# Eighteen runs of transposes in an attention stage taken from TensorE and done by VectorE in blocks of 32 and through DRAM

## The chip, the core and the metric

The program runs on one core of a Trainium2 chip. The core has a matrix engine (TensorE, PE in the profile, its weight loads PEld), a vector engine (VectorE, DVE), an activation engine (ScalarE, ACT), a general engine (GpSimd, POOL) and SyncE (SP), which here issues DMAs and relays semaphores. Every engine takes its own instructions strictly in the order in which they were written. The metric is device time in microseconds (us) of one execution; the number for the kernel before is the median of three runs.

## The reference, cut to what matters

The computation is four layers of a residual network over x, float32, 8 blocks of 512 tokens by 128 features. Each layer is an attention-like part and a feed-forward part, each behind a layer norm. The change is in the stage that does the attention of layer 2, together with what was folded into that stage: the expert layer of layer 2 (on the first 1024 tokens) and the whole of layer 3.

```python
# layer 2, attention: 16 heads of 64, softmax over the QUERIES (axis 2)
q, k, v = (einsum('bsd,hpd->bhsp', x, w) + bias for each)
scores  = einsum('bhqp,bhkp->bhqk', q, k) / 8
attn    = softmax(scores, axis=2)
ctx     = einsum('bhqk,bhkp->bqhp', attn, v)
out     = ctx.reshape(..., H * P) @ l_w.T + l_b
# layer 3, first part: a causal depthwise convolution of 21 taps
h_hatt  = conv(x, taps)
out     = x @ W1 + h_hatt @ W2 + bias
# layer 3, second part: both operands of every product rounded to FP4 in blocks of 16
gate, y = fp4(x) @ fp4(w_gate).T, fp4(x) @ fp4(w_up).T
out     = fp4(silu(gate) * y) @ fp4(w_down).T

x = x + L2_attn(layernorm(x));  x = x + L2_ffn(layernorm(x))
x = x + L3_attn(layernorm(x));  x = x + L3_ffn(layernorm(x))
```

Every product needs its input with the features on the partitions, while x lies with the tokens on the partitions. So each normalised block has to be transposed ("turned") before the product: 512 x 128 as four squares of 128.

## The kernel before, in words

`late()` (from L1403) holds the stage. It consists of 64 *frames*, n = 0 to 63: frame n is one pair of heads of one block of 512 tokens, eight frames to a block, so block 0 has frames 0 to 7, block 1 frames 8 to 15, and so on. In one frame the engines do, in the order written:

- `scores(n, 0)`: TensorE makes the scores of key tiles 0 and 1 (two PSUM pairs, `bank2`, of which there are two). VectorE takes the maxima (`nm`, L1626), ScalarE the exponentials (`ex`, L1632).
- `context(n - 1)`: TensorE multiplies the previous frame's exponentials with the weighted values.
- `scores(n, 1)`: key tiles 2 and 3. They need the two PSUM pairs back, that is, the exponentials of tiles 0 and 1 done.
- `project(n)`: TensorE makes queries, keys and values for later frames and the output product of the frame before; VectorE and ScalarE move `k`, `v` and `q` out of PSUM, `k` and `q` from the two banks of the pool "one".
- `weigh(n, 0)` and `weigh(n, 1)`: VectorE takes the reciprocals of the sums (`sm`, L1646), GpSimd scales the values.

Everything else is hung into these frames by a plan written out by hand. `at(frame, hook, f)` puts a step at one of six places of a frame; steps of one place run in the order in which they were entered, first the layer-2 inputs, then layer 3 of block 0, of block 1, and so on. The places: S between the score products of key tile 1; P between the exponentials of the two tiles; V after the first scores and before `context`; G before the second scores; D before the projections; E at the end of the frame, after `weigh(n, 1)` and before the next frame's scores. 

`planned(b, f0)` enters layer 3 of block b from frame f0 on, with f0 = 13, 20, 27, 34, 41, 48, 56 for blocks 0 to 6; block 7 comes in `end()`. Blocks 0 to 4 are "wide". Its steps before the change, by frame counted from f0: 0 statistics of the norm; 1 the norm (`scale`, ScalarE, four instructions) and the turn (`turn_`); 2 to 4 the taps of the convolution on VectorE, ScalarE and GpSimd; 5 its product, its sum into x and the second norm's statistics; 6 the second norm; 8 and 9 the rounding of x (`quant_x1`, `quant_x2`) and its turn (`turn_x`); 10 to 13 the gate and up products of the four tiles (`gate_steps`, hook S); 11 to 14 the rounding of h in two halves, each of 704 columns (`quant_h1`, `quant_h2`); 12 and 14 the turning of h (`blocks_h`), 13 and 15 its fetch (`fetch_h`), 16 the last product (`down`, three squares a tile). So in any run of seven frames, work of three blocks overlaps.

A *turn* is four transposes on TensorE against a unit matrix into one PSUM bank of the pool "one", and a copy of that bank (128 x 512) to SBUF, by ScalarE for activations and by VectorE for the weights. It stands at hook E, between `project` and the next frame's scores.

The turning of h is already done the other way: VectorE transposes 128 x 704 in blocks of 32 (L2151), four DMAs on the queue of SyncE write the blocks to their places in a DRAM array (L2155), and a frame later two DMAs bring back the rows (L2163).

SyncE has a second role. `mark` (L1518 to L1522) puts an instruction into SyncE's queue that waits for a matmul and then releases a later one; `project` has two of them in a frame and `gate_steps` one. A matmul that has such a mark ahead of it cannot start before SyncE has worked off all that stands before the mark.

## Time and profile before

| | |
|---|---|
| median of 3 runs | 1401.11 us (1397.96 to 1403.28) |
| the profiled execution | 1403.74 us, its span 1402.0 us |
| first and last exponential of the 64 frames start at | 514.3 us and 1337.8 us |
| seven frames of the middle, 938.70 to 1026.75 us | 88.05 us |
| TensorE, VectorE, ScalarE, GpSimd busy | 95%, 72%, 72%, 46% of the span |
| granted TensorE clock | 0.995 |

Times in the profile count from the start of the span. The busy share of TensorE is of modelled ends: the product of one group starts while the one before still drains, so that the start of the next group tells more than the end of this one. A line of the time order reads: start, duration, engine, line of the kernel, operation, out<-in, shape, count, and in brackets how long the engine had been idle and who ended that. The queue of SyncE is SPq. A DMA's "us to landing" is from its issue to the semaphore that tells its arrival.

### The profile page before, as it was taken

The page shows a single profiled execution, that of the slowest core. Times are in us where ns is not written, and L with a number is a line of the kernel's source. Part 1 is how long each engine was busy: PE and PEld are TensorE (multiplying, and loading weights), DVE is VectorE, ACT ScalarE, POOL GpSimd, SP SyncE. Part 2 cuts the span into 40 slices and gives each one's busy share as a digit, 9 for nine tenths or more (in the row PEclk, how much of TensorE's full clock was granted, in tenths as well). Part 3 has the DMA queues.
Part 4 walks back from the last instruction along what each step waited for, and adds up shares of the span by engine and source line. Part 5 has one row for each costly group of instructions (what it writes and reads, how often), then busy time and mean ns, then how long its engine had stood idle before and what let it go on. Part 6 is the DMA issues. An engine that isn't in the chain of part 4 may idle for free.

```text
span 1402.0 us, 33150 instructions
## 1 busy us (share of the span) xinstructions
PE 1336.6 (95%) x12967; PEld 711.6 (51%) x12967; DVE 1013.3 (72%) x2148; ACT 1011.9 (72%) x2052; POOL 647.0 (46%) x756
## 2 busy tenths in 40 slices
PE   7889999999989999999999999999999999999997
PEld 3762222222267655547446545555555555545576
DVE  6775655676467768863784678879788797887876
ACT  6859999999978555665685686777777767667632
POOL 6756666666632533340463354353443534424432
PEclk9999999999999999999999999999999999999999
DMA  5029999888581010021211101101001010010000
GB/s 179 1 40 130 132 136 133 128 124 126 79 271 31 28 40 24 17 82 30 82 32 43 45 1 23 23 10 33 20 18 27 9 33 20 12 33 9 2 8 16
DMA packets 84714, 78.15 MB, mean 56 GB/s; under 512 B 35821, under 2 KB 76685, under 8 KB 80078
## 3 DMA queue, kind: packets, MB, share of 16 engines
q1 hardware_dynamic: 82828, 72.10, 27.3%
q0 software_dynamic: 1152, 2.36, 0.6%
q8 instruction: 103, 1.69, 0.5%
q10 hardware_dynamic: 578, 1.57, 0.3%
q14 instruction: 53, 0.43, 0.1%
HBM read 59.03 MB, written 16.97 MB: 54 GB/s over the span
## 4 chain that ended last, share of the span: by engine, by line
PE 50%; ACT 23%; DVE 18%; DMA 3%; issue 3%; POOL 2%; SPq 1%; DVEq 0%; ACTq 0%; POOLq 0%
PE ps L250 39%; PE ps L1553 8%; ACT hm L568 7%; ACT ex L1632 6%; DVE nm L1626 5%; ACT hm L567 3%; ACT prod L2020 2%; DMA gs<-gates 2%; DMA gates<-eq 1%; PE ps L2203 1%; DVE fa L1392 1%; DVE acc L2006 1%; ACT h L388 1%; DVE s L729 1%; DVE fa L1376 1%
## 5 line engine op out<-in xcount | busy, mean ns | idle before, releaser
L1632 ACT ACTIVATE ex<-ps,nm 128x512 f32<-128x512 f32 x512 | 345.2, 687 | 173.6 <-DVE nm L1626 171.2
L1626 DVE TENSOR_REDUCE nm<-ps 128x2 f32<-128x1024 f32 x256 | 301.2, 1211 | 44.0 <-PE ps L250 43.6
L250 PE MATMUL ps<-q,k 64*64 64x512 f32 (+1 forms) x2240 | 259.5, 568 | 7.4 <-ACT ex L1632 5.4
L250 PE MATMUL ps<-ex,vs 128*64 128x512 f32 x1024 | 233.8, 598 | 1.1 <-DVE sm L1646 1.1
L1647 POOL TENSOR_TENSOR vs<-v,sm 128x256 f32<-128x256 f32 x128 | 78.6, 614 | 297.5 <-DVE sm L1646 268.2
L586 POOL TENSOR_TENSOR acc<-acc,pr 128x512 f32<-128x512 f32 x119 | 166.5, 1399 | 105.7 <-DVE pr L580 97.4
L1553 PE MATMUL ps<-xt,blob_a 64*64 64x512 f32 x912 | 208.0, 589 | 0.3 <-SPq L1520 0.2
L568 ACT ACTIVATE hm<-ps,blob_f 128x1536 f32<-128x1536 f32 x128 | 196.2, 1533 | 0.0
L580 DVE SCALAR_TENSOR_TENSOR pr<-ps,blob_f,gs 128x512 f32<-128x512 f32 x120 | 90.0, 750 | 88.2 <-PE ps L250 71.7
L250 PEld LDWEIGHTS ps<-q,k 64*64 64x64 f32 x2240 | 74.9, 132 | 151.0 <-ACT ex L1632 77.5
L250 PE MATMUL ps<-h,w 32*128 32x512 f32 x1024 | 147.4, 639 | 1.5 <-ACT hm L567 0.6
L250 PEld LDWEIGHTS ps<-ex,vs 128*64 128x64 f32 x1024 | 68.0, 136 | 153.7 <-issue 128.1
L250 PE MATMUL ps<-hm,w 128*32 128x512 f32 x1024 | 136.2, 604 | 3.2 <-DVE pr L580 3.0
L2021 POOL TENSOR_TENSOR acs<-acs,prod 128x512 f32<-128x512 f32 x96 | 124.1, 1292 | 23.9 <-ACT prod L2020 19.4
L1553 PE MATMUL ps<-blob_a,ct 64*64 64x128 f32 x1824 | 118.6, 269 | 0.0
L1553 PE MATMUL ps<-blob_a,xt 64*64 64x128 f32 x1824 | 118.5, 269 | 0.0
L1553 PEld LDWEIGHTS ps<-blob_a,ct 64*64 64x64 f32 x1824 | 106.1, 133 | 0.0
L1632 ACT ACTIVATION_READ_ACCUMULATOR ex<-ps,nm 128x1 f32 x512 | 105.0, 205 | 0.0
L1553 PEld LDWEIGHTS ps<-blob_a,xt 64*64 64x64 f32 x1824 | 103.0, 133 | 0.0
L567 ACT ACTIVATE hm<-ps,blob_f 128x512 f32<-128x512 f32 x128 | 88.0, 687 | 18.6 <-PE ps L250 18.5
L250 PEld LDWEIGHTS ps<-h,w 32*128 32x128 f32 x1024 | 40.7, 183 | 109.0 <-ACT hm L567 92.2
L1553 PEld LDWEIGHTS ps<-xt,blob_a 64*64 64x64 f32 x912 | 61.6, 132 | 32.3 <-issue 28.7
(375 smaller groups left out, 2219.9 us busy)
## 6 DMA issues: line engine op xcount, KB each, us to landing
gs<-gates SPq DMA_DIRECT2D x256, 128.0 KB, 6.7
ht<-turned_h SPq DMA_DIRECT2D x20, 180.0 KB, 2.9
turned_h<-hb SPq DMA_DIRECT2D x40, 88.0 KB, 2.3
blob_f<-in_f SPq DMA_DIRECT2D x1, 2560.0 KB, 9.3
blob_a<-in_a SPq DMA_DIRECT2D x1, 2056.0 KB, 15.4
x<-in_x SPq DMA_DIRECT2D x8, 256.0 KB, 5.6
gates<-eq SPq DMA_DIRECT2D x8, 256.0 KB, 5.6
slots_in<-nought SPq DMA_DIRECT2D x8, 256.0 KB, 4.3
```

The costliest lines, as they stand in the source:

```text
L250: nc.tensor.matmul(out_, lhs, rhs, start=start, stop=stop)
L388: nc.scalar.activation(hk, hk, AF.Sigmoid, bias=bi[:, k : k + 1], scale=sc[:, k : k + 1])
L567: nc.scalar.activation(hm[:, 0, :], p1, AF.Gelu, bias=bias)
L568: nc.scalar.activation(hm[:, 1:, :], p3, AF.Gelu, bias=bias)
L580: nc.vector.scalar_tensor_tensor(pr, po, f0["b2"][:, e : e + 1], gs, ALU.add, ALU.mult)
L586: nc.gpsimd.tensor_tensor(acc[:, b, :], acc[:, b, :], pr, ALU.add)
L1553: ins = nc.tensor.matmul(*args, **kw).ins
L1626: nc.vector.tensor_reduce(nm, ps, AX.X, ALU.max, negate=True)
L1632: nc.scalar.activation(ex[kt][:, i, :], ps[:, i, :], AF.Exp, bias=nm[:, i : i + 1], accum_out=sm[:, kt, i : i + 1],)
L1647: nc.gpsimd.tensor_tensor(vs[:, tiles, :, :], vs_[n][:, tiles, :].rearrange("p j (i n) -> p j i n", i=2), sm[:, tiles, :].unsqueeze(3).to_ ...
L2020: nc.scalar.activation(p, src, AF.Copy, scale=w)
L2021: nc.gpsimd.tensor_tensor(t["acs"], t["acs"], p, ALU.add)
```

## The change

Eighteen turns lose their transposes on TensorE and their copy out of PSUM: the inputs of layer 2 for blocks 1 to 7, the inputs of layer 3 for blocks 2 to 4, the rounded x of blocks 0 to 4, and the three rounded weights. In their place VectorE transposes the source in place in blocks of 32, four DMAs on SyncE's queue write it to a new DRAM array, and, one frame later (two for the weights), a DMA on the same queue fetches it.

```diff
+            def in_blocks(src):
+                nc.vector.transpose(src, src)
+                far = tc.dram_tile([P, TB], F32, name=f"turned{len(fars)}")
+                fars.append(far)
+                to = far.rearrange("(c r) (j a s) -> a r j c s", c=4, j=J, a=4)
+                for a in range(4):
+                    nc.sync.dma_start(
+                        to[a],
+                        src[32 * a : 32 * (a + 1), :].rearrange("r (j c s) -> r j c s", j=J, c=4),
+                    )
+                return far
...
+                def blocks():
+                    t["far"] = in_blocks(t["xn"].rearrange("p j d -> p (j d)"))
+
+                def fetch():
+                    nc.sync.dma_start(dst(), t["far"])
...
+                def blocks_x():
+                    t["far"] = in_blocks(t["xq"])
+
+                def fetch_x():
+                    t["xt"] = xt = tile_("xt", block("xt3", 2))
+                    nc.sync.dma_start(xt, t["far"])
...
-                plan = [
-                    (1, "V", s.stats) if b == 1 else (0, "E", s.stats),
-                    (1, "G", s.scale),
-                    (1, "E", s.turn_),
+                more = 2 if b < NB - 4 else 0
+                if 2 <= b <= 4:
+                    plan = [
+                        (-1, "E", s.stats),
+                        (0, "G", s.scale),
+                        (0, "E", s.blocks1),
+                        (1, "E", s.fetch1),
+                    ]
...
-                    (6, "E", s.quant_x1) if early else (z - 2, "V", s.quant_x1),
-                    (z - 1, "V", s.quant_x2),
-                    (z - 1, "E", s.turn_x),
+                if wide:
+                    plan += [
+                        (z - 3, "V", s.quant_x1),
+                        (z - 2, "V", s.quant_x2),
+                        (z - 2, "E", s.blocks_x),
+                        (z - 1, "E", s.fetch_x),
+                    ]
...
-                    (h_ + 4, "V", lambda: s.quant_h2(1)),
+                    (h_ + 4 + more, "V", lambda: s.quant_h2(1)),
...
-                        (z + 4, "E", lambda: s.blocks_h(1)),
-                        (z + 5, "E", lambda: s.fetch_h(1)),
-                        (z + 6, "E", s.down),
+                        (z + 4 + more, "E", lambda: s.blocks_h(1)),
+                        (z + 5 + more, "E", lambda: s.fetch_h(1)),
+                        (z + 6 + more, "E", s.down),
...
-                at(n + 1, "E", turn_)
+                for i, f in enumerate(t_["in turn"]):
+                    at(n + 1 + i, "E", f)
...
-                    at(frame + 1, "E", lambda name=name: turned_w(name))
+                    at(frame + 1, "E", lambda name=name: raw.update({(name, 0): turned_w(name)}))
+                    at(frame + 3, "E", lambda name=name: fetch_w(name, raw[name, 0]))
```

(z is 10 for the wide blocks.) Around these, three more things move. For layer 3 of blocks 2 to 4 the statistics and the norm come one frame earlier, into frames f0 - 1 and f0. The rounding of x of the wide blocks comes one frame earlier, into frames f0 + 7 and f0 + 8. And for blocks 0 to 3 the second half of h is rounded, turned, fetched and multiplied (`down`) two frames later: rounding and `blocks_h(1)` in f0 + 16 instead of f0 + 14, `down` in f0 + 18 instead of f0 + 16. The statistics and norms of the layer-2 inputs stay where they were.

## Prediction

> **What bounds the kernel now.** I read the page first (busy shares, chain), then the seven frames that repeat in the middle, then the time order of each engine at the places that the change touches.
>
> ```profile
> span 1402.0 us, 33150 instructions
> PE 1336.6 (95%) x12967; PEld 711.6 (51%) x12967; DVE 1013.3 (72%) x2148; ACT 1011.9 (72%) x2052; POOL 647.0 (46%) x756
> PE 50%; ACT 23%; DVE 18%; DMA 3%; issue 3%; POOL 2%; SPq 1%; DVEq 0%; ACTq 0%; POOLq 0%
> ...
> 953.86:966.03 12.17, 12.17 (x136) 5.98 (x134) 10.75 (x24) 8.92 (x25) 3.07 (x7) 1.00 0.12 33
> 966.03:977.73 11.70, 11.61 (x136) 5.96 (x134) 10.86 (x23) 8.92 (x25) 5.27 (x8) 1.00 0.13 20
> 977.73:988.23 10.50, 10.41 (x130) 5.61 (x128) 8.05 (x13) 8.80 (x24) 3.10 (x7) 1.00 0.22 50
> 988.23:1002.83 14.60, 14.15 (x176) 9.27 (x176) 11.26 (x16) 10.57 (x25) 4.60 (x5) 1.00 0.07 21
> ```
>
> The four stretches are frames 33 to 36, from first exponential to first exponential: length, then PE, PEld, DVE, ACT, POOL busy (instructions), clock, DMA. TensorE fills 97 to 100% of each; VectorE 77 to 93%, ScalarE 72 to 84%. In block 3's count (f0 = 34) they are f0 - 1 to f0 + 2. So TensorE is the bound, but a chain of maxima, exponentials and freed PSUM runs close behind it: what is added to VectorE or ScalarE is hidden only by a microsecond or so.
>
> ```profile
> 972.91 0.49 PE L1553 MATMUL ps<-blob_a,xt 64*64 64x128 f32 x6
> 973.51 0.63 PE L1469 MATMUL ps<-blob_c,xn 128*128 128x128 f32 x4
> 974.07 1.95 PE L250 MATMUL ps<-q,k 64*64 64x512 f32 x16
> ...
> 997.09 2.94 PE L250 MATMUL ps<-wd,ht 120*128 120x128 f32 x24 [0.45 <-DVE k L1515]
> 999.87 0.60 PE L2086 MATMUL ps<-blob_c,fa 128*128 128x128 f32 x4
> 1000.40 1.52 PE L250 MATMUL ps<-q,k 64*64 64x512 f32 x16
> 1001.74 0.46 PE L2203 MATMUL ps<-wt_gate,xt 64*64 64x352 f32 x2
> 968.69 0.60 ACT L1667 COPY ct<-ps 128x512 f32<-128x512 f32 x1
> 969.16 1.66 ACT L1451 ACTIVATE xn<-x,nb,rs 128x128 f32<-128x128 f32 x4
> 970.71 0.40 ACT L1964 ACTIVATE tapw<-blob_l 128x128 f32<-128x128 f32 x1
> 971.14 0.69 ACT L1632 ACTIVATE ex<-ps,nm 128x512 f32<-128x512 f32 x1
> ...
> 975.29 2.03 SPq L2155 DMA_DIRECT2D turned_h<-hb  x4
> L2151 DVE STREAM_TRANSPOSE hb<-h x10: 877/880/882, 861.0 to 1240.1; 128x704 f32<-128x704 f32 x10
> DMA to landing us min/median/max: 1.9/2.3/3.8
> rows<-back SPq DMA_DIRECT2D x7, 256.0 KB, 2.7
> ```
>
> To see: a turn (L1469, L2086) takes 0.53 to 0.56 us from its start to the next product's. In frame 34 ScalarE goes from copy to norm to tap weight to exponential without a gap. Four block writes hold SyncE's queue 2.03 us (L2155). The gate product of a block begins 1.34 us after the scores of its frame (1001.74 against 1000.40).
>
> **Term 1, TensorE's turns: -13.3 us.** After a projection a turn costs 0.56 and some 0.27 more (the last projection group starts 0.60 before the turn, 0.33 before scores where no turn stands): 0.83. After `down` only 0.53. Layer-2 inputs 7 x 0.83 = 5.85; layer-3 inputs 3 x 0.83 = 2.5; rounded x 0.9 + 4 x 0.53 = 3.0; three weights about 0.64 each = 1.9. With them go 15 ScalarE copies of 0.58; the three weight copies on VectorE (0.49 to 0.53) are replaced by transposes.
>
> **Term 2, VectorE's transposes: 0 by themselves.** 704 columns take 0.88; the rounding's rows of 352, 512 and 704 columns (0.53, 0.69, 0.89) give 1.0 ns a column, so 0.68 for 512 (bounds 0.49, a copy of 352 columns, and 0.88). At hook E VectorE waits up to 0.75 for the next scores in the lighter frames, and these now come 0.83 earlier; I charge the heavy frames in term 4.
>
> **Term 3, a DMA that comes too late: 4 x 5.3 = +21.2 us.** `fetch_x` stands at E of f0 + 9, one frame before its reader: the gate product in f0 + 10. With `down` moved, `blocks_h(1)` of the block before (its f0 + 16) falls into the same hook E, and it was entered first. This is so in frames 29, 36, 43 and 50; the built order of SyncE's queue has there four `turned_h<-hb`, then `xt<-turned`, then the gate's mark. So `fetch_x` waits behind four writes, which wait for a VectorE transpose at the very end of the frame. From the end of the frame's last exponential, e: `sm` 0.17, `hb` 0.88, four issues 2.05, then the fetch. No row has this 256 KB fetch; I take `rows<-back`, 256 KB from DRAM, 2.7 (bounds 2.2, the `out<-x` store, and 3.5, the slowest `ht` fetch). Landing is at e + 5.9 to 6.4, the longer where VectorE is late with `v`. TensorE wants the gate product at about e + 0.8, when `q` (0.70 on ScalarE after e) has freed its bank; `down` and `turn_x`, 3.3 us before, no longer stand ahead of it. So it stands 5.3 us (4.3 to 6.1), in order, and with it the rest of the scores, `context`, the tanh and the exponentials behind it. Nothing of that is cover: the reader is TensorE.
>
> Block 0's fetch (frame 22) has no writes before it, is issued in the middle of the projection and lands about when the gate wants it: 0. `fetch1` has a frame of convolution start to wait for it (f0 + 2, V), behind four writes of `blocks_x`: 0 to 0.5, taken 0. The eight writes of f0 hold SyncE about 4.1 us; the next marks are those of `project`, some 7 us after E: 0.
>
> **Term 4, VectorE and ScalarE in f0 - 1 to f0 + 1 of blocks 2 to 4: 3 x 2.2 = +6.6 us.** The statistics (0.84 + 0.36 + 0.17, overlapped 1.23) now stand before the next maxima in f0 - 1, where another 1.23 already stands: exponentials 1.2 later, second scores about 1.0 later. In f0 ScalarE, which has no gap, gets a second norm of 1.65: the second exponentials start at about 973.9 instead of 971.14 (frame 34), and the scores of the next frame need the PSUM that they free. Four exponentials (2.7) and the last tile's scores (0.85) later these scores end at 977.5 instead of 975.95, although the turn is gone. The rounding of h that leaves f0 (2.85 us of VectorE) and the copies that go give about 1.0 back in f0 + 1. So of two turns (-1.66) nothing is left, and 0.55 is added: 2.2. Bounds 0 (all in the shade of TensorE) and 3.2.
>
> **Term 5, VectorE in f0 + 9: 4 x 1.4 = +5.6 us.** There the rounding of 704 columns (0.53 + 0.53 + 0.89 + 0.89) takes the place of 512 (0.42 + 0.43 + 0.69 + 0.69), before two taps and the second maxima, and `hb` comes at the end; also `blocks_x` in the frame before. That is 0.61 more, on top of the 0.55 that term 4 left and a transpose of 0.68 just before: the second maxima come 1.2 to 1.7 later than without, and the last exponentials with them. Bounds 0 and 1.7.
>
> **Term 6, the rest: -0.2 us.** `down` in f0 + 18 stands where TensorE starts scores 0.45 earlier than ScalarE, busy with taps, can use them: 0.45 less, 0.27 more for the step from a projection to it, 4 x -0.2. Frame 21: statistics of block 1 come behind `quant_x2` (2.23) instead of `quant_x1` (1.90), with a transpose at E: +0.6.
>
> Sum: -13.3 + 21.2 + 6.6 + 5.6 - 0.2 = +19.9. Against the profiled execution's 1403.74 that is 1423.6; this execution lies 2.6 above the median of its three runs, so against the median I say 1421.0.
>
> **A rule of the Trainium skill.** The page "VectorE: DVE Perf Modes", section "Rules for kernel authors", speaks against the change: a 128 x 128 transpose belongs on TensorE if PSUM will do as its destination. Its section "The three transpose paths" gives 390 ns there for one such square of bf16. The row here is 0.56 us for four squares of float32. By the page's figure 18 turns would free 28 us, an estimate, and the sum would be +5; by the rows it is 13.3.
>
> **Rivals.**
> *A, faster, 1388 to 1394.* TensorE is the bound and gets its 13.3 us, or 7 of them, whole. For it: 97 to 100% busy in frames 33 to 36. It needs `fetch_x` to land within 0.8 us of e, that is, writes that don't stand before it in the queue; the built order says they do. The point where it decides is the landing of that fetch against the gate's scores.
> *B, about the same, 1400.* The fetch is in time after all (TensorE some 5 us later than I think, because term 5 is larger), and terms 4 and 5 eat the turns: -13.3 + 6.6 + 5.6 - 0.2 = -1.3. Against it: both sides start from the same exponentials.
> *C, much slower, 1440.* SyncE's writes take the longest row of one (1.645) instead of the mean 0.51: eight in f0 would take 13 us and hold the marks of the next projection some 6 us, in three frames, on top of the forecast (+18). Against it: four of them take 2.03 to 2.06 in all three places that I looked at.
> That the change doesn't do what it says is out: the built queues have the transposes, the writes and the fetches, and 60 + 9 products less.
>
> **How the numbers follow.** Forecast 0.82, A 0.05, B 0.08, C 0.05. What a measurement of this kernel tells from no change is 0.5%, 7 us: 1394 to 1408. Faster 0.05 (A); same 0.10 (B, and the lowest of the forecast); slower 0.85. With the low ends (4.3 at the gates, terms 4 and 5 at nothing) the sum is +3, with the high ends (6.1, 3.2, 1.7 and a third of term 1 lost) about +32: 1404 to 1433. I give 1407 to 1433.
>
> **What would show it.** In frames 30, 37, 44 and 51 the first gate product (L2230 or near) waits some 5 us for DMA `xt<-turned`, and that DMA's issue follows four `turned_h<-hb` without a gap: term 3. If the wait is under 2, the forecast is wrong. Frames 27, 34 and 41 longer than 11 us though a turn is gone: term 4. No wait of TensorE for SyncE in frames 28, 35 and 42, or C is right. Frames 2 to 8 shorter by about 4 us together: term 1 where nothing stands against it.

## The result, and the profile after

The changed kernel takes 1446.18 us (median of six runs, 1445.18 to 1451.93), the kernel before beside it 1400.32 (six runs): a ratio of 1.034, interval 1.032 to 1.036. The direction was forecast; the time lies 25 us above the forecast 1421.0 and 13 above the end of its range. The profiled execution took 1445.78 for a span of 1444.0.

First the page of the changed kernel: span, busy times, and the shares of the chain of waits.

```profile
span 1444.0 us, 33198 instructions
PE 1335.1 (92%) x12898; PEld 704.4 (49%) x12898; DVE 1020.2 (71%) x2163; ACT 1005.3 (70%) x2037; POOL 646.2 (45%) x756
PE 39%; DVE 11%; ACT 9%; DMA 2%; issue 2%; SPq 2%; POOL 1%; ACTq 0%; DVEq 0%; POOLq 0%
```

TensorE has 69 products less and only 1.5 us less of busy time, which is the first sign that something slowed its products down; its idle time went from 65 to 109 us. So I counted the frames of layer 2, each from its first exponential to the next frame's. They are worth more than the medians here: everything ahead of frame 0 is the same code in all kernels, and took from 508.7 to 518.6 us in the seventeen profiled executions, while a frame that is the same in two kernels mostly agrees to 0.05 us. In the frames the change costs 47.0 us, in the medians 45.9.

The table compares the forecast, sorted by the frames in which its terms fall, with the frames of the two profiles.

| frames | what the change does there | forecast, us | measured, us |
|---|---|---|---|
| 2 to 6 | weights, block 1's input | -2.7 | -3.1 |
| 7 to 9 | block 2's input; copy of the down weights | -0.8 | +13.9 |
| 10 to 19 | block 3's input | -0.8 | -0.3 |
| 20 to 25 | block 0's rounded input | -0.3 | -0.4 |
| 26-28, 33-35, 40-42 | layer 3's inputs, layer 2's of blocks 4 to 6 | +1.6 | +3.5 |
| 29-32, 36-39, 43-46, 50-53 | rounded inputs, `down`, gate product | +23.9 | +33.6 |
| 47-49 and 54 on | block 7's input | -0.8 | -0.2 |
| all | | +20 | +47.0 |

Two rows make the miss. The first is frame 7, where the forecast had only a turn less. The stretches of the changed kernel's trace there, in the time order of SyncE's DMA queue, of VectorE and of TensorE (start, length, engine, line, operation; in brackets the idle time before it and what ended it):

```profile
594.82 2.61 SPq L1436 DMA_DIRECT2D turned<-xn  x4
598.58 0.39 SPq L1796 DMA_DIRECT2D oa<-in_byrow  x1
...
604.86 0.63 SPq L2503 DMA_DIRECT2D wd<-turned_down  x1
594.07 0.68 DVE L1431 STREAM_TRANSPOSE xn<-xn 128x512 f32<-128x512 f32 x1
608.00 0.27 DVE L2504 MEMSET wd<- 4x256 f32 x1 [13.26 <-DMA wd<-turned_down]
608.21 2.27 DVE L1646 TENSOR_REDUCE nm<-ps 128x2 f32<-128x1024 f32 x2
595.01 3.65 PE L250 MATMUL ps<-ex,vs 128*64 128x512 f32 x16
610.95 3.69 PE L250 MATMUL ps<-q,k 64*64 64x512 f32 x16 [12.29 <-ACT ex L1652]
```

A memset of four rows, 0.27 us of work, stands on VectorE for 13.26 us. It clears the overlap in the third copy of the down weights and must come after what writes them. In the kernel before that was VectorE's own copy out of PSUM; now it is a DMA, and the memset stands with it in the step that fetches, two frames later. That DMA is issued only at 604.86, behind block 2's four transposed writes and eight loads of expert weights. The maxima of the next scores stand behind the memset, the exponentials behind the maxima, and TensorE waits 12.29 us; then sixteen score products take 3.69 where they take 1.95 elsewhere.

The second is the gate product. Frames 33 to 38 of the changed kernel (columns as in the stretches before: length, busy PE, PEld, DVE, ACT, POOL, clock, DMA share, GB/s):

```profile
969.12:982.54 13.42, 13.42 (x142) 6.41 (x140) 11.97 (x33) 8.92 (x25) 4.16 (x10) 1.00 0.11 30
982.54:994.42 11.88, 10.04 (x124) 5.00 (x122) 9.19 (x15) 9.85 (x27) 4.66 (x7) 1.00 0.04 7
994.42:1004.74 10.32, 10.32 (x128) 5.49 (x126) 8.84 (x14) 7.03 (x20) 2.29 (x4) 1.00 0.41 72
1004.74:1017.46 12.72, 9.54 (x124) 5.04 (x120) 11.88 (x16) 9.96 (x24) 4.80 (x5) 1.00 0.24 45
1017.46:1036.40 18.94, 14.76 (x176) 7.98 (x176) 8.85 (x13) 10.56 (x26) 7.34 (x8) 0.82 0.24 52
1036.40:1051.05 14.65, 14.65 (x180) 9.17 (x176) 10.34 (x15) 10.50 (x26) 10.60 (x11) 1.00 0.06 17
```

Frame 33 is 1.25 us longer than before (statistics of layer 3's input), frame 36 shorter because `down` (2.8 us) went to frame 38, frame 37 6.85 longer, with a granted clock of 0.82. In the time order of the changed kernel around the end of frame 36 (SyncE's queue, VectorE, TensorE):

```profile
1016.31 2.11 SPq L2182 DMA_DIRECT2D turned_h<-hb  x4
1018.55 0.46 SPq L2108 DMA_DIRECT2D xt<-turned  x1
1015.41 0.88 DVE L2178 STREAM_TRANSPOSE hb<-h 128x704 f32<-128x704 f32 x1
1013.89 1.09 PE L250 MATMUL ps<-q,k 64*64 64x512 f32 x8 [1.36 <-ACT ex L1652]
1015.23 0.66 PE L250 MATMUL ps<-q,k 64*64 64x256 f32 x8 [0.25 <-ACT ex L1652]
1021.64 0.85 PE L2230 MATMUL ps<-wt_gate,xt 64*64 64x352 f32 x2 [5.75 <-DMA xt<-turned]
```

This is term 3 as forecast: the fetch follows four writes without a gap, the writes follow the transpose of `hb`, and the gate product waits 5.75 us for it. What was not forecast is in the next view, three stretches after each other: the wait, the gate products with the scores between them, and the context products.

```profile
1015.50:1021.64 6.14, 0.39 (x9) 0.03 (x1) 1.89 (x2) 3.41 (x8) 4.40 (x4) 0.70 0.56 103
1021.64:1024.94 3.30, 3.30 (x25) 1.41 (x25) 0.94 (x1) 0.00 (x0) 0.00 (x0) 0.53 0.00 0
1024.94:1028.52 3.58, 3.58 (x20) 1.06 (x16) 2.83 (x6) 1.80 (x5) 0.19 (x1) 1.00 0.02 5
```

After the wait TensorE has a granted clock of 0.53, and this stretch, 1.73 us at clock 1.00 in the kernel before, takes 3.30.

### The profile page after: what moved, and what is told of

It is laid out like the page before. It is cut to its first block, busy times and chain, and to the rows that moved or that the text cites. A ratio compares the mean times of both kernels' runs of the same rounds, so it can differ in the third digit from the quotient of the medians.

```text
span 1444.0 us, 33198 instructions
## 1 busy us (share of the span) xinstructions
PE 1335.1 (92%) x12898; PEld 704.4 (49%) x12898; DVE 1020.2 (71%) x2163; ACT 1005.3 (70%) x2037; POOL 646.2 (45%) x756
## 4 chain that ended last, share of the span: by engine, by line
PE 39%; DVE 11%; ACT 9%; DMA 2%; issue 2%; SPq 2%; POOL 1%; ACTq 0%; DVEq 0%; POOLq 0%
PE ps L250 28%; PE ps L1573 9%; ACT ex L1652 5%; DVE nm L1646 3%; PE ps L2230 2%; ACT xn L1464 1%; DVE acc L2026 1%; DMA xt<-turned 1%; DMA xp<-turned 1%; DVE v L1520 1%; ACT prod L2040 1%; DVE s L1452 1%; SPq L1436 1%; SPq L2182 1%; DVE fa L1376 0%
## 5 line engine op out<-in xcount | busy, mean ns | idle before, releaser
L250 PE MATMUL ps<-q,k 64*64 64x512 f32 (+1 forms) x2240 | 265.7, 576 | 33.4 <-ACT ex L1652 31.1
L2041 POOL TENSOR_TENSOR acs<-acs,prod 128x512 f32<-128x512 f32 x96 | 123.5, 1286 | 16.1 <-ACT prod L2040 11.6
```

Of the source, the lines that this page charges most:

```text
L250: nc.tensor.matmul(out_, lhs, rhs, start=start, stop=stop)
L2041: nc.gpsimd.tensor_tensor(t["acs"], t["acs"], p, ALU.add)
```

## The experiments

Fifteen kernels. The table gives the medians, the ratio to the kernel before with its interval, and what the frames of the profiled execution took more or less than before (the third group is the nine frames with layer 3's inputs, the fourth the sixteen around the gate product). They ran on four chips (E1 to E4, E5 to E8, E9 to E12, E13 to E15), each kernel beside the kernel before. On the chip of E5 to E8 frame 12 alone is 2.0 to 2.2 us longer in each; the column "all" holds that.

| kernel | us | ratio | 2-6 | 7-9 | nine | sixteen | all |
|---|---|---|---|---|---|---|---|
| changed | 1446.2 | 1.034 (1.032-1.036) | -3.1 | +13.9 | +3.5 | +33.6 | +47.0 |
| E1 memset later | 1439.8 | 1.027 (1.024-1.031) | -3.1 | +6.0 | +3.5 | +32.5 | +36.7 |
| E2 fetch earlier | 1424.5 | 1.018 (1.014-1.022) | -3.1 | +13.9 | +3.5 | +8.7 | +21.9 |
| E3 both | 1417.2 | 1.012 (1.009-1.016) | -3.1 | +6.1 | +3.5 | +10.8 | +15.0 |
| E4 42 idle products | 1457.1 | 1.039 (1.036-1.043) | -3.1 | +14.2 | +4.3 | +40.3 | +54.8 |
| E5 no delay | 1449.9 | 1.034 (1.029-1.040) | -3.1 | +14.1 | +13.3 | +16.3 | +44.1 |
| E6 E3, layer 3's inputs on TensorE | 1413.1 | 1.007 (1.005-1.010) | -3.1 | +6.0 | -1.0 | +9.3 | +11.6 |
| E7 writes on ScalarE's queue | 1426.9 | 1.019 (1.014-1.023) | -3.1 | +14.4 | +3.5 | +10.6 | +28.5 |
| E8 22 idle products | 1439.7 | 1.027 (1.022-1.031) | -3.1 | +14.1 | +3.6 | +24.8 | +41.0 |
| E9 ten turns | 1400.2 | 0.999 (0.997-1.001) | -3.1 | 0.0 | +1.4 | -0.1 | -3.3 |
| E10 delay alone | 1425.8 | 1.017 (1.014-1.021) | 0.0 | 0.0 | -0.4 | +25.8 | +24.9 |
| E11 E9 and the inputs | 1403.1 | 1.003 (1.001-1.005) | -3.1 | 0.0 | +8.3 | -3.7 | +3.4 |
| E12 E11 and the delay | 1406.7 | 1.003 (1.001-1.006) | -3.1 | 0.0 | -1.0 | +7.5 | +3.0 |
| E13 five turns | 1397.2 | 0.997 (0.995-0.999) | -3.1 | 0.0 | -0.5 | -0.1 | -4.6 |
| E14 later inputs alone | 1401.4 | 1.001 (0.999-1.003) | 0.0 | 0.0 | +1.3 | 0.0 | +1.7 |
| E15 E1, down weights fetched earlier | 1438.9 | 1.027 (1.023-1.031) | -3.1 | +5.4 | +3.3 | +32.4 | +36.2 |

(Frame 40 of the profile of before is itself 0.44 longer than in E9 and in E11 to E14, which leave it alone; so the nine frames' zero lies at -0.4. Frame 22 is some 1.2 shorter in E1, E3, E5, E6, E9 and E15 than in the other kernels that turn block 0's input in blocks: that is TensorE's clock in this one execution and not the edit, as the last section shows.)

### E1: the memset moved

```diff
                         nc.sync.dma_start(wt["down"][:C3], three)
-                        nc.vector.memset(wt["down"][: C3 - thirds[1][1], 1:, :], 0.0)
...
+                def no_overlap():
+                    nc.vector.memset(wt["down"][: C3 - thirds[1][1], 1:, :], 0.0)
+
+                at(11, "E", no_overlap)
```

> The changed kernel with one step moved: the memset that clears the overlap of the third copy of the down weights goes from frame 7's E to frame 11's E; its DMA stays where it is. Theory: in the changed kernel the whole of frame 7's +13.4 us is VectorE standing 13.26 us at this memset for a DMA that SyncE issues only at 604.86, behind the expert weights and four transposed writes, and TensorE standing with it (12.29 us at the scores, then 3.5 us for scores that take 1.77 elsewhere, at a granted clock of 0.50). By frame 11 the DMA landed long ago, so 13.4 us go: 1446.2 - 13.4 = 1432.8 us (1431 to 1435), frame 7 again 15.1 us shorter or longer by under 1, no clock record of 0.5 near 601. Rival 1: the weights' own rounding and transposes on VectorE in frames 4 to 7 are what is late, and the memset only shows it: frame 7 keeps at least half of its 13 us and the time stays above 1439. Rival 2: SyncE's queue is what is late, and the next user of a DMA in frames 8 to 10 (the rows' weights) stands in the memset's place: frame 7 is mended, frames 8 to 10 grow by 5 us or more, 1437 to 1446.

1439.75 us, 6.4 less instead of 13.4. Frame 7 is mended to 0.13 us, as the theory had it; but frame 8 is 5.46 longer than before the change and frame 9 0.66: rival 2's kind of loss, with another reader than it named. SyncE's queue and TensorE of E1:

```profile
599.56 2.61 SPq L1436 DMA_DIRECT2D turned<-xn  x4
...
610.29 0.63 SPq L2503 DMA_DIRECT2D wd<-turned_down  x1
606.38 0.60 PE L1573 MATMUL ps<-xt,blob_a 64*64 64x512 f32 x2
611.04 1.12 PE L1573 MATMUL ps<-xt,blob_a 64*64 64x512 f32 x2 [4.01 <-SPq L1540]
```

L1540 is the mark with which SyncE lets the second half of a projection start. It stands in the same queue, behind everything that was late in frame 7, and TensorE waits 4.01 us for it; the projection then runs at half speed (1.12 for a pair that takes 0.60). Before the memset was moved, VectorE's stall covered this one.

### E2: the fetch of the turned inputs moved

```diff
-                        (z - 1, "E", s.fetch_x),
+                        (z - 1, "D", s.fetch_x),
```

> The changed kernel with one step moved: the fetch of the turned, rounded inputs of blocks 0 to 4 goes from the E place of frame f0+9 to the D place of the same frame, which puts it ahead of the four writes of the hidden block (turned_h<-hb) in SyncE's queue. Theory: in the changed kernel the fetch of frame 36 is issued at 1018.55 behind the four writes (1016.31 to 1018.12) and lands at 1021.50, the gate product stands 6.12 us for it, and then runs 3.30 us instead of 1.73 at a granted clock of 0.53. With the fetch at about 1010 it lands at about 1013, before the product is due at 1015.5: 4 x (6.1 + 1.6) = 30.8 us go, 1446.2 - 30.8 = 1415.4 us (1411 to 1418); frames 30, 37, 44, 51 each 5 to 8 us shorter, no clock record of 0.5 in blocks 1 to 4. Rival 1: VectorE's longer work in these frames is what holds the gate product and the DMA merely ends last: a VectorE or ScalarE wait of 3 us or more takes the DMA's place, 1425 to 1440. Rival 2: the write of the hidden block, now later by one fetch, is late for the down product: frames f0+17 of the earlier block grow by 1 us or more each, 1419 to 1424.

1424.54 us, 21.6 less in the medians and 25.1 in the frames; frames 30, 37, 44 and 51 are 6.9, 5.7, 6.0 and 5.9 shorter, so the wait is gone, but 6 us a block came back and not 7.7. SyncE's queue and TensorE of E2:

```profile
1001.84 0.33 SPq L2108 DMA_DIRECT2D xt<-turned  x1
1010.34 2.05 SPq L2182 DMA_DIRECT2D turned_h<-hb  x4
1010.33 0.75 PE L250 MATMUL ps<-q,k 64*64 64x256 f32 x8
1012.50 0.51 PE L2230 MATMUL ps<-wt_up,xt 64*64 64x352 f32 x2 [1.42 <-SPq L1540]
```

The fetch goes out 8.5 us ahead of the writes. Now the second half of the gate product waits 1.42 us, again for SyncE's mark, which stands behind the four writes. That is what keeps frame 37 1.14 us longer than before.

### E3: both

> Both moves of the two kernels beside it. Theory: the two waits are apart in place and cause, and add: 1446.2 - 13.4 - 30.8 = 1402.0 us (1397 to 1406), so the turns taken from TensorE (forecast 13.3 us) are given back almost in full by VectorE's longer frames (forecast 12.2 us in terms 4 and 5). Rival: nothing but the two waits cost anything, terms 4 and 5 are hidden, and the change is worth its turns: 1400.3 - 13.3 = 1387 us (1384 to 1392). Rival: with both waits gone another one shows (the fetch of block b's layer-3 inputs, 1.25 us in frame 36): 1407 or above.

1417.2 us, against 1402 by the theory. The two do add (in the frames 10.3 and 25.1 alone, 32.0 together), but each gives back less than its wait: 6.2 us stay in frames 8 and 9, and 10.8 around the gates. Of these 2.5 belong to frame 51 of this execution, where the wait for the mark is 2.21 us instead of 1.43 and the context products after it run at half clock. The rival that saw nothing but the two waits (1387) is out; the last one, another wait behind these two, is what came, though at the marks and not at the fetch that it named.

### E4 and E8: TensorE kept at work in the wait

```diff
                     def first():
+                        if j == 0 and 1 <= b <= 4:
+                            keep_clock(42)
                         t["gate", j] = pg, pu = bank(), bank()
```

`keep_clock(n)` issues n products of the identity with itself, which nobody reads; E8 is the same with 22.

> The changed kernel with nothing moved, but 42 products of the identity with itself ahead of the first gate product of blocks 1 to 4 (about 0.11 us each at full clock by layer 0's products of that size, so some 4.6 us of the 6.1 us in which TensorE stands for the fetch). Their result is read by nobody. Theory: the wait ends when it did (the fetch lands at about 1021.5 in frame 37), and the second half of the loss is the clock: granted 0.53 after the idle time, so that the gate stretch takes 3.30 us instead of 1.73. With TensorE kept at work it stays at 1.0: 4 x 1.6 = 6.4 us go, 1446.2 - 6.4 = 1439.8 us (1438 to 1442), and the clock records of 0.5 near 816, 922, 1018, 1113 are gone or shorter. Rival 1: the low clock is no matter of idle time (it comes with the time since something else, or with the transfer): the stretch still takes 3.3 us, 1446 to 1448. Rival 2: the idle products take longer than the wait, or a bank of theirs is missing: 1448 or above.

> As the run with 42 identity products, but with 22 of them: those took 9.57 us for 42 (0.228 each) and so were longer than the wait of 6.1 us; 22 take 5.0. In that run the granted clock stayed at 1.00 and the gate stretch took 1.89 us (3.30 at 0.53 without them). Theory: the wait ends when it did in the changed kernel, the stretch takes 1.9 instead of 3.3 at a clock of 1.00, so frames 30, 37, 44, 51 are each 1.4 to 1.6 us shorter than in the changed kernel: 1446.2 - 6 = 1440 us (1437 to 1443 for medians). Rival: the idle second that is left before the gate product is enough for the clock to fall, and the stretch takes over 2.5 us: 1443 to 1447.

E4 ended at 1457.1: I had taken 0.11 us for a product that is recorded as two of that length, so 42 took 9.57 us and outlasted the wait. E8, with 22 and two runs only, is at 1439.7, 6.5 under the changed kernel, and 8.8 under it in the sixteen frames. The stretches of E8 in frame 37, the idle products and the gate products:

```profile
1016.56:1022.42 5.86, 5.18 (x49) 5.02 (x45) 1.57 (x2) 3.10 (x7) 4.18 (x4) 1.00 0.61 108
1022.42:1024.14 1.72, 1.72 (x24) 0.86 (x24) 0.41 (x1) 0.00 (x0) 0.00 (x0) 1.00 0.00 0
1022.42 0.51 PE L2230 MATMUL ps<-wt_gate,xt 64*64 64x352 f32 x2 [0.68 <-DMA xt<-turned]
```

The product still waits for the same DMA, but the clock is 1.00 and the stretch takes 1.72 instead of 3.30. With nothing else changed, this shows that the second part of these losses is the clock after an idle TensorE.

### E5: the hidden half not delayed

```diff
-                more = 2 if b < NB - 4 else 0
+                more = 0
```

> The changed kernel with the two-frame delay of the second hidden half undone (quant_h2(1), blocks_h(1), fetch_h(1) and down of blocks 0 to 3 in the frames that the kernel before has them in); the fetch of the turned inputs stays at E of frame f0+9. Theory of the queue: the four writes turned_h<-hb then go out in frame f0+7 of the next block and nothing stands ahead of the fetch in frame f0+9, so the gate waits (4 x 7.7 us) go as with the earlier fetch, and also the 1.42 us in which the gate's second half stood behind these writes for SyncE's mark: 1446.2 - 30.8 - 4 x 1.3 = 1410 us (1407 to 1414). Rival of VectorE: quant_h2(1) now meets quant_x1 in frame f0+7, both on VectorE, and the frames f0+7 and f0+8 grow by 1 us or more in four blocks: 1414 to 1420. Rival: the fetch is late at place E whatever stands ahead of it, and the gate still waits 3 us or more: 1425 or above.

1449.9: no better than the changed kernel. Frames 27, 34, 41, 48 are 2.8 to 3.2 us longer than before the change (quantisation of h and of the inputs on VectorE, and in SyncE's queue twelve writes one after another, from 997.61 at the end of frame 34 to 1006.63), as the rival of VectorE said; and the gate still waits. SyncE's queue and TensorE of E5 around the end of frame 36:

```profile
1024.62 0.41 SPq L2221 DMA_DIRECT2D out<-x  x1
1025.21 0.36 SPq L2108 DMA_DIRECT2D xt<-turned  x1
1027.96 0.51 PE L2230 MATMUL ps<-wt_gate,xt 64*64 64x352 f32 x2 [2.64 <-DMA xt<-turned]
```

At place E the fetch is now behind the store of `down`'s output, which cannot be issued before `down` has run. So the last rival was right too, at 2.6 us where it had 3: at place E of this frame the fetch is late behind either step.

### E7: the writes on another queue

```diff
+                    queue = nc.scalar if i and b < NB - 3 else nc.sync
                     for a in range(4):
-                        nc.sync.dma_start(to[a], src[a])
+                        queue.dma_start(to[a], src[a])
```

> The changed kernel with nothing moved in time: only the four writes of the second hidden half (blocks 0 to 4) are issued on ScalarE's queue instead of SyncE's. Theory: what made the fetch of the turned inputs late is its place in SyncE's queue behind these writes, which wait for VectorE's transpose at 1016.31; with them on another queue it goes out some 7 us earlier at the same place E. 4 x 7.7 us go, and 4 x 1.3 for SyncE's mark of the gate: 1446.2 - 36 = 1410 us, plus what the four issues cost ScalarE (0.3 to 0.54 us each on SyncE, so up to 2 us in four blocks): 1410 to 1418. Rival: the fetch is late because of the data (VectorE's rounding of the inputs), and the queue is innocent: the gate wait stays, 1440 or above. Rival: ScalarE stands for VectorE's transpose and the exponentials behind it come late by more than 3 us a block: 1422 or above.

1426.9 us. Of E7, ScalarE's queue and SyncE's:

```profile
1012.32 2.06 ACTq L2183 DMA_DIRECT2D turned_h<-hb  x4
1007.15 0.33 SPq L2108 DMA_DIRECT2D xt<-turned  x1
```

The fetch, at its old place E, goes out 5 us before the writes; the gate wait and the wait for the mark are gone, and frame 37 is 1.5 us shorter than before. So the queue is the cause. But ScalarE, which stands 2.67 us at these issues, makes frame 36 2.8 us longer than in the changed kernel: in sum no better than the moved fetch (+10.6 in the sixteen frames against +8.7), and what the last rival said.

### E6: layer 3's inputs on TensorE

```diff
-                if 2 <= b <= 4:
-                    plan = [
-                        (-1, "E", s.stats),
-                        (0, "G", s.scale),
-                        (0, "E", s.blocks1),
-                        (1, "E", s.fetch1),
-                    ]
-                else:
-                    plan = [
...
-                    ]
+                plan = [
+                    (1, "V", s.stats) if b == 1 else (0, "E", s.stats),
+                    (1, "G", s.scale),
+                    (1, "E", s.turn_),
+                ]
```

The diff is against E3.

> The kernel with both moves (memset later, fetch earlier), and with layer 3's inputs of blocks 2 to 4 turned on TensorE again in the frames of the kernel before. It prices term 4 (forecast 3 x 2.2 us less the turns removed, 3 x 0.83, so a net of 4.1). By the frames of the changed kernel, blocks 2 to 4 lost 1.45, 1.24 and 0.81 us in frames f0-1 to f0+1, 3.5 together; and the fetch xp<-turned landed 1.25 us too late for the convolution in frame f0+2. Theory: both go, 3.5 us in the first frames and up to 3 x 0.8 in frames f0+2: 1417.2 - 5 = 1412 us (1409 to 1415). Rival: the late xp is hidden (the exponentials behind it have room), 1417.2 - 3.5 = 1413.7, frames f0+2 the same to 0.1 us. Rival: the transposes are free and the loss in these frames comes from the longer queue of SyncE: 1416 to 1419.

1413.1 us, 4.1 under E3 (on another chip; 3.4 in the frames). The three groups of frames f0 - 1 to f0 + 1 gain 1.65, 1.37 and 1.47, and frames f0 + 2 another 0.35, 0.35 and 0.65: the late `xp` did cost something. Block 4's frame gained most, and there ScalarE of the changed kernel waits 2.91 us for `xp`, against 1.20 and 1.25 for blocks 2 and 3. Turned in blocks, with statistics a frame earlier, these three inputs are a loss of 5.8 us; on TensorE they cost nothing over before.

### E10: the delay without any turn in blocks

```diff
+                more = 2 if b < NB - 4 else 0
...
-                    (h_ + 4, "V", lambda: s.quant_h2(1)),
+                    (h_ + 4 + more, "V", lambda: s.quant_h2(1)),
...
-                        (z + 4, "E", lambda: s.blocks_h(1)),
-                        (z + 5, "E", lambda: s.fetch_h(1)),
-                        (z + 6, "E", s.down),
+                        (z + 4 + more, "E", lambda: s.blocks_h(1)),
+                        (z + 5 + more, "E", lambda: s.fetch_h(1)),
+                        (z + 6 + more, "E", s.down),
```

The diff is against the kernel before.

> The kernel before with nothing but the delay: quant_h2(1), blocks_h(1), fetch_h(1) and down of blocks 0 to 3 two frames later; all turns stay on TensorE. It shows what the delay costs without any turn in blocks. Theory: the four writes turned_h<-hb now stand in SyncE's queue ahead of the mark that lets the gate's second half start (1.42 us of TensorE waiting for SyncE in frames 30, 37, 44, 51 of the kernels with the earlier fetch), so those frames grow by about 1.1 each, and 2.8 us of down move from frames 29, 36, 43, 50 to 31, 38, 45, 52: 1401 + 4.5 = 1405.5 us (1404 to 1408). Rival: the mark is held only because VectorE is late with the rounded inputs' transpose; alone, the delay costs nothing: 1400 to 1402.

1425.8 us: 25 us more, where I expected 4.5. VectorE and TensorE of E10 in frame 36:

```profile
995.68 0.89 DVE L1392 TENSOR_TENSOR fa<-fa,fm 128x704 f32<-128x704 f32 x1
996.61 0.89 DVE L1393 TENSOR_TENSOR fa<-fa,fm 128x704 f32<-128x704 f32 x1
...
999.40 0.69 DVE L1392 TENSOR_TENSOR fa<-fa,fm 128x512 f32<-128x512 f32 x1
1000.12 0.69 DVE L1393 TENSOR_TENSOR fa<-fa,fm 128x512 f32<-128x512 f32 x1
...
1005.59 0.74 DVE L1515 TENSOR_SCALAR k<-ps,blob_a 128x512 f32<-128x512 f32 x1
1006.47 1.09 PE L2086 MATMUL ps<-blob_c,fa 128*128 128x128 f32 x4 [4.46 <-DVE k L1515]
```

The rounding of h (704 columns) and that of the inputs (512) now meet in one frame, the copy of `k` comes after both, and TensorE waits 4.46 us for it and then runs at clock 0.50. So the delay and the earlier quantisation of the inputs belong together: either alone makes VectorE the bound of one frame (E10 here, E5 and E11 in frames 27, 34, 41 and 48).

### E9, E11, E12: the turns sorted

E9 keeps ten turns (weights with the down copy fetched in frame 6 and the memset in frame 11; layer 2's inputs but block 2's; block 0's rounded input). E11 adds the rounded inputs of blocks 1 to 4 with the earlier fetch, E12 also the delay. E9 against E6:

```diff
-                more = 2 if b < NB - 4 else 0
+                more = 0
...
-                if wide:
+                if b == 0:
                     plan += [
                         (z - 3, "V", s.quant_x1),
...
-                for i, f in enumerate(t_["in turn"]):
-                    at(n + 1 + i, "E", f)
+                if b == 2:
+                    at(n + 1, "E", turn_)
+                else:
+                    for i, f in enumerate(t_["in turn"]):
+                        at(n + 1 + i, "E", f)
...
-                    at(frame + 3, "E", lambda name=name: fetch_w(name, raw[name, 0]))
+                    at(min(frame + 3, 6), "E", lambda name=name: fetch_w(name, raw[name, 0]))
```

E11 has `if wide:` again, E12 also `more` as it was.

> The kernel before with ten of the eighteen turns in blocks: the three weights (fetch of the down weights at E of frame 6, ahead of the expert weights in SyncE's queue; its memset at E of frame 11), layer 2's inputs of blocks 1 and 3 to 7, and the rounded input of block 0 (its fetch at D). The other eight (layer 2's inputs of block 2, layer 3's inputs of blocks 2 to 4, rounded inputs of blocks 1 to 4) are on TensorE and the second hidden half is not delayed. Theory, by the frames of the changed kernel: frames 2 to 6 -3.1, frames 7 to 9 as before (within 0.3), frames 15 and 16 -0.1, the four later inputs -0.2 each, frame 22 -0.6 to -2.0: -5.0 in all, 1401 - 5 = 1396 us (1393 to 1398), ahead of both kernels. Rival: the expert weights' loads, not block 2's turn, are what delays the marks of frame 8, and frames 7 to 9 keep 5 us: 1401. Rival: forecast term 1 at its own prices (3 x 0.64 + 6 x 0.83 + 0.9 = 7.8 us): 1393.

> The kernel with ten turns in blocks beside it, and the rounded inputs of blocks 1 to 4 too (fetch at D), without the delay of the hidden half. Theory: quant_h2(1) meets quant_x1 on VectorE in frame f0+7 (with the delay undone in the changed kernel, frames 34, 41, 48 grew by 2.7 to 3.0 us), so four times 2.7 less 0.5 for the turn: 8.8 us over the kernel beside it, 1405 (1402 to 1408). Rival: that loss came from SyncE, which there had eight transposed writes of layer 2's and layer 3's inputs in the same frame; here layer 3's inputs are back on TensorE, and the inputs in blocks are worth their turns: 1394.

> As the kernel beside it, with the delay of the hidden half (blocks 0 to 3) as the change has it. It is the whole change less layer 3's inputs and block 2's input, with the two late pieces (memset, fetch) mended. Theory: the gate's mark behind the four writes (1.1 us) and frame f0+9's longer VectorE and ScalarE work (1.1 us), less the turn (0.5): 1.7 us in four blocks, 6.9 over the kernel with ten turns, 1403 (1401 to 1406). The delay is then the cheaper of the two, by some 2 us. Rival: the delay's cost is all in the mark and nothing in frame f0+9: 1399.

E9: 1400.2, the same as before; in the frames 3.3 us less, not the 5.0 expected, and 1.2 of the 3.3 are the clock in frame 22. Frames 7 to 9 are as before to 0.02 us, so the expert weights by themselves are innocent. Frames 27, 34, 41 and 48 are 0.6 longer each. E11 (1403.1) and E12 (1406.7) are both slower by 0.3%; in the frames they cost 6.7 and 6.3 over E9 (5.5 and 5.1 without frame 22's clock), where 8.8 and 6.9 were expected. The delay is not the cheaper of the two by more than these runs can tell. What E12 loses around a gate is 1.1 us to the mark in frame f0 + 10, and 1.1 in frame f0 + 9: with `down` (2.8 us) left aside that frame is 0.6 longer, though a turn of 0.53 is gone from it.

### E13, E14, E15: the two open pieces

E13 is E9 without layer 2's inputs of blocks 3 to 7 (one condition of E9, `if b == 2`, became `if b > 1`). E14 is the kernel before with layer 2's inputs of blocks 4 to 7 in blocks, nothing else. E15 is E1 with the `min(frame + 3, 6)` of E9.

> The kernel before with five of the turns in blocks: the three weights (down weights fetched at E of frame 6, memset at E of frame 11), layer 2's input of block 1 and the rounded input of block 0 (fetch at D). Theory, by the frames of the kernel with ten: frames 2 to 6 -3.1, frames 20 to 23 -1.8, and the +0.6 in frames 27, 34, 41 and 48 gone, since nothing is turned in blocks there: -4.9 us in the frames, 1400 - 4.9 = 1395 us (1392 to 1398). Rival: the gain in frames 20 to 23 belongs to the later inputs' other order and goes too: -3.1, 1397. Rival: what the frames gain is lost outside them, as it seemed with ten turns: 1400.

> The kernel before with four turns in blocks alone: layer 2's inputs of blocks 4 to 7 (turned in frames 27, 34, 41, 48). By the forecast's term 1 they are worth 4 x 0.83 = 3.3 us: 1397. Theory after the runs: in those frames VectorE also turns the second hidden half, SyncE carries eight writes instead of four, and 0.6 us are lost in each: 1400 + 2.4 = 1402 us, frames 27, 34, 41, 48 each 0.5 to 0.7 longer. Rival: the +0.6 comes from layer 3's inputs or rounded inputs of other blocks, and here the four frames are 0.2 shorter each, as in the kernels with the delay: 1399.

> The changed kernel with the memset at E of frame 11 and the fetch of the down weights at E of frame 6, ahead of the expert weights; block 2's input is still turned in blocks in frame 7. With the memset moved alone, frame 7 was mended and frame 8 grew by 5.46 us, TensorE waiting 4.01 for SyncE's mark. Theory: the mark is held by block 2's four writes, which stand 3.4 us for VectorE's transpose and take 2.7 to issue, with the expert weights behind them; the copy of the down weights takes 0.63 of the queue: frame 8 stays 4.5 to 5.4 us longer, 1439 us. Rival: the copy waits for the turned weights or its own place behind the expert weights is what matters: frame 8 within 1 us of before, 1434 us.

E14: frames 27, 34, 41 and 48 are 0.6 longer each, and 1401.4 us in all (ratio 1.001): four turns fewer on TensorE are a small loss, where term 1 had a gain of 3.3. In these frames VectorE also turns the second hidden half and SyncE writes it. Frame 34 shows that VectorE is the cause: its rows in the kernel before (first exponential at 966.03) and, with TensorE's, in E14 (969.90):

```profile
974.39 0.88 DVE L2151 STREAM_TRANSPOSE hb<-h 128x704 f32<-128x704 f32 x1
976.41 2.35 DVE L1626 TENSOR_REDUCE nm<-ps 128x2 f32<-128x1024 f32 x2
...
977.12 1.90 PE L250 MATMUL ps<-q,k 64*64 64x512 f32 x16
978.26 0.68 DVE L1431 STREAM_TRANSPOSE xn<-xn 128x512 f32<-128x512 f32 x1
978.87 0.87 DVE L2172 STREAM_TRANSPOSE hb<-h 128x704 f32<-128x704 f32 x1
980.88 2.35 DVE L1647 TENSOR_REDUCE nm<-ps 128x2 f32<-128x1024 f32 x2
```

Counted from the first exponential, the score products begin at 7.22 us instead of 8.04 (974.07 in the prediction's lines): the 0.82 are the turn. But the maxima begin at 10.98 instead of 10.38. VectorE works without a gap up to them in both kernels, and in E14 it has the input to transpose ahead of `hb`. With the second hidden half two frames later (E12) the frames gain 0.0 to 0.2. E15: frame 8 still 4.6 longer; TensorE of E15:

```profile
607.12 1.12 PE L1573 MATMUL ps<-xt,blob_a 64*64 64x512 f32 x2 [3.18 <-SPq L1540]
```

With block 2's input on TensorE (E9) no such wait is left. So it is block 2's four writes, with the expert weights behind them, that hold the mark, and the down copy had only 0.8 us of frame 8 in it.

E13, the five turns of frames 2 to 5 and 21, is the only version ahead of the kernel before: 1397.19 us over twelve runs, ratio 0.997 (0.995 to 0.999), a gain that is just what twelve runs can tell. The frames have 4.6 us less where 4.9 were expected, but that agreement is partly luck. Frames 2 to 6 give the 3.1 expected; frames 20 to 23 give 0.6 and not 1.8, since 1.2 of E9's gain there was the clock; and 0.8 lie in frames 10 and 40, which E13 does not touch and which are shorter in E14 too (0.1 and 0.4). So the five turns are worth about 3.7 us. The span of the profiled execution, 1401.5 us, is no shorter than before's, because the unchanged part ahead of frame 0 took 518.6 us in it against 514.3.

## Why the prediction was wrong, point by point

**The step that failed** is the half sentence in term 1, "the three weight copies on VectorE (0.49 to 0.53) are replaced by transposes". They are replaced by transposes and, for the down weights, by a DMA with the old memset behind it, two frames later. I costed the transposes, left the memset's wait out, and put nothing for SyncE's queue in frame 7, where that DMA stands behind block 2's writes and the expert weights. Forecast for frames 7 to 9 was -0.8 us, measured +13.9: over half of the miss. With these frames at zero the time would have been 1432.3, just inside the range, but that is a sum and no run: moving the memset alone gives back 8.0 of the 13.9, since the wait for SyncE's mark was hidden under it (E1, 1439.8 us); with the memset later, the fetch earlier and block 2's input on TensorE all of it is gone (E9). Most of the rest of the miss, 9.7 us in the sixteen frames, is in term 3 and the marks below.

**Term 1, the turns (-13.3).** Right where the frames were light: frames 2 to 6 gave 3.1 for a forecast 2.7. Wrong for layer 2's later inputs: a gain of 0.83 each was forecast, and E14 shows a loss of 0.6 each without the delay, E12 a gain of 0.0 to 0.2 with it. The price of 0.83 was right (the scores begin 0.82 earlier), but the maxima on VectorE end those frames, as E14's rows show; the prediction named that chain as running "close behind" and then did not charge it there. (Two sums are slightly off: 7 x 0.83 is 5.81, and the low ends add up to +3.7, not +3. Nothing rests on either.)

**Term 2, the transposes (0).** The size was right; the rows of the changed kernel for the 512-column transposes, least, median and most ns:

```profile
L1431 DVE STREAM_TRANSPOSE fa<-fa x5: 679/679/680, 818.0 to 1196.7; 128x512 f32<-128x512 f32 x5
L1431 DVE STREAM_TRANSPOSE xn<-xn x10: 668/680/683, 562.0 to 1185.2; 128x512 f32<-128x512 f32 x10
```

0.68 us, as estimated. In the heavy frames they are not free: that is E14's 0.6.

**Term 3, the late fetch (+21.2).** The mechanism was right, down to the order of the queue (E2 and E7 take it away by moving the fetch or the writes). The first gate products of frames 30, 37, 44 and 51 wait 5.67, 5.75, 5.15 and 5.50 us, for a forecast 5.3. The term left out what follows a wait: gate products at clock 0.53, 1.6 us more in frame 37 (E8 gets 8.8 us back in the sixteen frames). E2 gets 24.8 us back there.

**Term 4 (+6.6, so +1.6 net of its turns).** Undersized: +3.5 in the nine frames, and E6 finds 5.8 with frames f0 + 2, where the fetch of `xp`, costed under term 3 at "0 to 0.5, taken 0", was 1.2 to 2.9 late. The 1.0 that was to come back in f0 + 1 came to 0.3 at most.

**Term 5 (+5.6).** About right: frame f0 + 9 is 0.6 longer in E6 and E12 with `down` left aside, which makes 1.1 us with the turn's 0.53, for a forecast 1.4. No run measures the 0.53 by itself.

**Term 6 (-0.2).** Frame 21 grew by 0.4 for a forecast 0.6; the slack under `down` did not show. Nothing rests on it.

**What no term had** is SyncE's mark in the gate frames, 1.1 us in four of them. It shows only once the fetch is in time (E2).

**The rivals.** A (the turns gained whole) needed the fetch in time; even with that and the memset mended, E3 stands 1.2% above before. B fell with it. C had the right kind of loss for the wrong reason: the four writes shown above took 2.1 to 2.6 us, not 6.6, and the frames f0 + 1 that it named show no wait for SyncE; yet SyncE's marks were held in frame 8 (4.0 us in E1) and in the gate frames (1.4 in E2).

**The rule weighed.** The Trainium skill's page "VectorE: DVE Perf Modes", section "Rules for kernel authors", has a full transpose on TensorE if PSUM will do. The runs agree for twelve of the eighteen; the five in E13 pay, with about 3.7 us together, and block 3's input is worth 0.1.

## What to carry to other kernels

When work leaves the bounding engine for DMAs, write down every instruction that the new step issues, a memset of four rows too, and for each one that waits for a DMA find what stands ahead of that DMA in its issuing queue: here two such places cost 14 and 25 us, while the turns that paid gave 3.7. Before a freed microsecond of the bounding engine is counted, look in that frame at which engine the next step really waits for. Put a fetch ahead of writes that wait for late data in the same frame, and look also at the marks that the queue relays, since mending one wait uncovers the next one in the same queue. Price a wait of TensorE of 3 us or more with the products that follow it at half clock.

## What the runs showed that I had not expected

TensorE's granted clock falls to 0.5 after waits, and the length of one wait does not decide it. After waits of 3.18 (E15), 4.01 (E1), 4.46 (E10), 5.75 and 12.29 us (changed kernel) the next products ran at 0.50 to 0.53 for about 3 us and more. Shorter waits go either way. One of 1.42 us (E2) and one of 2.64 (E5, frame 37: the gate stretch after it took 1.78) left it at 1.00. In E5 TensorE waits 2.55 us for the exponentials in frame 34 and again in frame 41: after the first the scores run at 0.54, after the second at 1.00.

The shortest are at the end of frame 21, where all kernels turn layer 3's input of block 1 on TensorE. In the kernel before TensorE waits there 1.26 and 0.84 us, with 0.63 us of products between; in E9 it waits 1.58 and 0.87. The score products that follow and the first context products, first in the kernel before, then in E9 (columns as in the stretches above):

```profile
810.87:814.44 3.57, 3.57 (x17) 0.72 (x17) 1.40 (x2) 2.60 (x7) 0.67 (x2) 0.52 0.00 0
807.57:809.92 2.35, 2.10 (x16) 0.41 (x16) 1.03 (x3) 2.33 (x6) 0.67 (x2) 1.00 0.00 0
```

These are the 1.2 us of frame 22. Half clock comes there in eleven of the seventeen profiled executions, in E13 too, whose edits up to this frame are those of E9 but for block 3's input. What decides it for such short waits, no run here shows.

The Trainium skill's page "TensorE: Matmul & The Clock Gate", section "Part 1: The HAM clock gate (the "warmup" mystery)", has the halving after an idle window of about 3.4 us and the return after as much work. The long waits agree with it in kind. The wait of 2.55 us in frame 34 and the pair in frame 21 are shorter than that window and were followed by half clock; there the measurement decides.

Filling the wait with products that nobody reads is worth it only if they end before it does: in the sixteen frames 22 of them (5.0 us) gained 8.8 us over the changed kernel, 42 (9.57 us) lost 6.7.
